# Four-quadrant rows and pixels, Hartley rows stored in their final layout, and a new order of the pieces

## The chip, the cores and the metric

The kernel runs on one core of a Trainium2 chip. The metric is the device time of the program in microseconds; lower is better. The engines named here are PE (matrix products, with PEld for its weight loads), ACT (activations and copies), DVE (vector operations), POOL (GpSimd) and SP, whose queue issues most of the DMA transfers. All data is float32.

## What is computed

Two layers follow each other on an input of 16 images, 64 channels, 128 by 128 pixels. The first is a Hartley convolution: a 2-d Hartley transform, a product with weights on 20 x 20 low modes, the transform back, a Gaussian blur over all four axes, and a mask on the columns. The second is an image network: group norm, a spectral mixer (AFNO) on 32 x 32 modes, a residual, a second group norm, one dense layer of features, two shared experts, and four of sixteen experts per image that a small gate chooses. Cut to what matters:

```python
def _L0_conv_ref(x, w1):
    x_ht = dht_2d(x)
    out_ht = out_ht.at[:, :, :M1, :M2].set(compl_mul2d(x_ht[:, :, :M1, :M2], w1))
    y = gaussian_smoothing_4d(dht_2d(out_ht) / (H * W))
    return y * mask

def _forward(x, ...):
    h = _afno(_group_norm(x, gn1_w, gn1_b), afno_w1, afno_b1, afno_w2, afno_b2) + x
    residual = h
    feats = _gelu(_c1(_group_norm(h, gn2_w, gn2_b), fe_w, fe_b))
    for s in range(shared_w.shape[0]):
        shared = shared + _gelu(_c1(feats, shared_w[s], shared_b[s])) / shared_w.shape[0]
    scores = h2 @ g3_w.T + g3_b          # h2: the gate's layers on the mean of feats
    vals, idx = jax.lax.top_k(scores, TOP_K)
    wts = jax.nn.softmax(vals / TEMPERATURE, axis=1)
    out = shared
    for e in range(NUM_EXPERTS):
        out = out + _gelu(_c1(feats, expert_w[e], expert_b[e])) * gate_w[:, e][:, None, None, None]
    return out + residual
```

## The kernel before

**Stage 1, the transform forward (lines 187 to 266).** Each image is read in eight tiles `xt` and transformed along rows (L250) and, one image later, along columns (L212). DVE adds the result, with the blur over the batch, into `x2` (L231). When an output image is complete, ACT writes its two other halves of `x2` (L236 with a sign, L237 as a copy). The stage is a stream from DRAM of about 330 GB/s.

**Stage 2, modes (lines 268 to 321).** Constants are loaded, `spec` (3.2 MB) and `exw` among them. Eleven steps mix channels per mode (L294) into PSUM tiles `psm`, of which there are two. Each is copied to the two halves of `om`: the lower half by ACT (L298, L301, L302), the upper by DVE (L299, L303). L312 turns them into `ot`, 400 modes in four chunks by image and channel.

**Stage 3, the AFNO loop over 16 images (lines 324 to 567).** After the statistics, every image has eight products of `spec` (L548) and the first layer (L499, L501), whose result goes to DRAM as `o1d` (L503, SP). In the first ten rounds `modes` (L480, L483) also builds `ok`, the Hartley rows of all images on 4 x 32 partitions; in the next four `modes_out` makes a negated copy `onk` (L488) and stores both on POOL's queue to `od` and `ond` (L490, L491), 32 stores of 100 KB with 5,120 B in a row. `prepare` folds the constants; it also makes two rows of bias, `b2r`, and stores them to `b2x`.

**Stage 4, the pieces (lines 570 to 889).** Every image is now worked through in pieces:

- `spectrum` (lines 602 to 611) loads `s` from `o1d` (L606), and the Hartley rows into columns 64 to 104 of `bm` by eight loads (L611). Each row of 20 values is a packet of 80 B.
- `spectrum_f`, twice: 64 products of the second AFNO layer (L622) into one PSUM tile, copied to columns 0 to 63 of `bm` by ACT (L629).
- `rows`, eight times: four channels, four products each (L647), copied to `u` by ACT (L652).
- `pixels`, eight times: for eight rows one product of 107 x 128 x 128 each (L669); ACT adds the residual's shift and writes `h` (L677), DVE takes statistics (L681).
- `norm2` (three steps), `feature` (eight, L732 and L736), and `gate` (eight steps), which ends in a softmax on POOL and DVE and in four gathers of expert weights `wl` (L806).
- `group`, 48 times: four products of 64 x 64 x 512 (L826), a gelu by ACT into `g` (L831), and an addition by DVE into `h` (L834), two shared and four chosen experts for each of eight tiles. After the last expert of a tile its two halves are stored (L845).

All pieces share three PSUM tiles, `pe`, of two banks each. An evacuation is put one piece behind its products, and an addition one further. `PIECES` (line 872 on) holds for each piece its places, counted in groups: piece i of image b stands at `b * 48 + at`, so that a place of -50 means two groups before the end of the image before. The pieces are written out in that order; the framework then orders each queue by what is ready, earlier code first.

```python
        PIECES = (
            (lambda box, i: spectrum(box), (-84,)),
            (spectrum_f, (-57, -50)),
            (feature, (-5, -4, -3, -2, -2, -2, -2, 0)),
            (step("norm", norm2), (-19, -16, -10)),
            (step("gate", gate), (2, 3, 5, 7, 8, 8, 10, 12)),
            (rows, (-50, -49, -48, -48, -48, -40, -39, -38)),
            (pixels, (-36, -32, -28, -24, -24, -24, -23, -23)),
            (group, range(NG)),
        )
```

Of the kernel before, what the change touches and what calls it, by code (L numbers as in the profile page):

```python
# [19 lines left out]
K = 20  # L20
# [9 lines left out]
HR, KC = 52, 105  # L30
KU = KC + 2
# [23 lines left out]
def constant_tables():  # L55
# [23 lines left out]
    inv1, inv2 = np.zeros((128, 2, N)), np.zeros((KU, N))  # L79
# [7 lines left out]
    inv2[KC], inv2[KC + 1] = inv2[:32].sum(0), inv2[32:64].sum(0)  # L87
    c, s = np.cos(a32).sum(0), np.sin(a32).sum(0)
    bias = np.array([[c, s], [-s, c]])

    by_half = lambda t: t.reshape(-1, 2, 2, N // 2).transpose(0, 1, 3, 2).reshape(-1, 2 * N)
    inv1, bias = by_half(inv1), by_half(bias)
# [38 lines left out]
    for loc in range(5):  # L131
# [13 lines left out]
        "bias": bias,  # L145
# [14 lines left out]
def hartley_afno_moe_kernel(ctx: ExitStack, tc: tile.TileContext, a: dict, out: bass.AP):  # L160
# [18 lines left out]
    od = dram.tile([NB, K, C, K], F32, name="od")  # L179
    ond = dram.tile([NB, K, C, K], F32, name="ond")  # L180
# [6 lines left out]
    with tc.tile_pool(name="modes", bufs=1) as mp:  # L187
# [6 lines left out]
        with tc.tile_pool(name="f_x", bufs=10) as xp, tc.tile_pool(name="f_t", bufs=2) as tp, \  # L194
# [9 lines left out]
            def along_columns(b, t1):  # L204
# [20 lines left out]
                for bo in range(NB):  # L225
# [9 lines left out]
                    if not gb[bo, b + 1:].any():  # L235
                        nc.scalar.mul(x2[0:C, 1, bo], x2[C:P, 0, bo], -1.0)  # L236
                        nc.scalar.copy(x2[C:P, 1, bo], x2[0:C, 0, bo])  # L237
# [39 lines left out]
        spec = load(sc, "spec", [CH, 4, 2 * MD * MD])  # L277
        exw = load(sc, "exw", [P, C, NE])

        with tc.tile_pool(name="m_o", bufs=1) as op, \  # L280
# [7 lines left out]
            for k1 in range(K // 2 + 1):  # L288
# [9 lines left out]
                nc.scalar.copy(lok[:, k1], lo[:, :, 0])  # L298
                nc.vector.tensor_copy(upk[:, k1], up[:, :, 0])  # L299
                if k1 % (K // 2):  # L300
                    nc.scalar.copy(lok[:, K - k1, 0:1], lo[:, 0:1, 1])  # L301
                    nc.scalar.copy(lok[:, K - k1, K // 2 - 1:0:-1], lo[:, 1:, 1])  # L302
                    nc.vector.tensor_copy(upk[:, K - k1, ::-1], up[:, :, 1])  # L303
# [18 lines left out]


# [10 lines left out]
    b2 = kp.tile([2, C], F32, name="b2t")  # L334
    for ri in range(2):
        nc.sync.dma_start(b2[ri:ri + 1], a["b2"][32 * ri:32 * ri + 1, 0:C])
    bias = load(kp, "bias", [2, 2, N])
    b2r = kp.tile([P, 2, C], F32, name="b2r")
    b2x = dram.tile([2, N, C], F32, name="b2x")
    inv1 = load(kp, "inv1", [P, 2, N])  # L340
    inv2 = load(kp, "inv2", [KU, N])
# [20 lines left out]
    bm = kp.tile([P, CL, KC], F32, name="bm")  # L362
    nc.gpsimd.memset(bm, 0.0)
# [7 lines left out]
    with tc.tile_pool(name="s_w", bufs=2) as sw, tc.tile_pool(name="s_o", bufs=1) as so, \  # L371
# [15 lines left out]
        ok = so.tile([P, QB, C, K], F32, name="ok")  # L387
        onk = so.tile([P, QB, C, K], F32, name="onk")
        nc.gpsimd.memset(onk, 0.0)
# [83 lines left out]
        def modes(m):  # L473
# [3 lines left out]
            for i in range(2):  # L477
# [6 lines left out]
                ok[:, :, :, 2 * m:2 * m + 2].rearrange("p b c k -> p k (b c)"), ps,  # L484
                st.unsqueeze(1).to_broadcast([P, 2, QB * C]), ALU.mult)

        def modes_out(i):
            nc.scalar.mul(onk[:, i, :, 0:K - 1], ok[:, i, :, 1:K], -1.0)  # L488
            for q in range(4):
                nc.gpsimd.dma_start(od[q * QB + i], ok[q * 32:q * 32 + K, i])  # L490
                nc.gpsimd.dma_start(ond[q * QB + i], onk[q * 32 + 1:q * 32 + 1 + K, i])  # L491
# [14 lines left out]
        def prepare():  # L506
# [8 lines left out]
            ps = pp3.tile([P, 512], F32, name="pso")  # L515
            for i in range(2):
                nc.tensor.matmul(ps[:, i * C:(i + 1) * C], lhsT=bias[:, i], rhs=b2, start=True, stop=True)
            nc.scalar.copy(b2r.rearrange("p i c -> p (i c)"), ps[:, 0:2 * C])
            nc.sync.dma_start(b2x.rearrange("i n c -> n i c"), b2r)
# [50 lines left out]
    with s3:  # L570
        up_, hpp, fp, gp, selp = (pool(n, q) for n, q in (
            ("u", 1), ("hp", 14), ("feats", 9), ("g", 7), ("selw", 2)))
# [5 lines left out]
        nc.sync.dma_start(u[KC:KU], b2x)  # L578
# [22 lines left out]

        def spectrum(box):

            b = box["b"]
            s = box["s"] = sp.tile([P, MD * MD], F32, name="s")
            nc.sync.dma_start(s, o1d[b].rearrange("r c k -> (r c) k"))  # L606
            for h in range(2):
                r, i = (0, 32) if h else (64, 96)
                cs = slice(h * CL, (h + 1) * CL)
                for at, q, src in ((r, 0, od), (i, 1, od), (r + 1, 21, od), (i, 21, ond)):  # L610
                    nc.sync.dma_start(bm[at:at + K, :, 64 + q:64 + q + K], src[b, :, cs, :])  # L611

        def spectrum_f(box, q):
# [13 lines left out]
            def evacuate():  # L627
                bmf = bm[:, :, 0:64].rearrange("p c (r j) -> p r c j", r=2)
                nc.scalar.copy(bmf[:, :, :, q * 16:(q + 1) * 16], ps.rearrange("p i r c -> p r c i"))  # L629
                if q:  # L630
                    box["spectrum"] = True
# [3 lines left out]
        def rows(box, q):  # L635


            if q == 0:
                if "spectrum" not in box:
                    flush()  # L640
            ps = ps2.tile([P, 2, 4, N], F32, name="pe")
            for i in range(4):
                for part, h in ((0, 0), (1, 0), (0, 1), (1, 1)):
                    k0 = C * (h ^ part)
                    rs = slice(k0, k0 + (HR if part else C))
                    cs = slice(64, KC) if part else slice(0, 64)
                    nc.tensor.matmul(ps[cs, h, i, :], lhsT=bm[rs, 4 * q + i, cs],  # L647
                                     rhs=inv1[rs, part], start=True, stop=True)

            def evacuate():  # L650
                dst = u[0:KC].rearrange("p n (h s) -> p h s n", h=2)[:, :, 4 * q:4 * q + 4, :]
                nc.scalar.copy(dst.rearrange("p h s n -> p n h s"),  # L652
                               ps[0:KC].rearrange("p h s n -> p n h s"))
# [4 lines left out]
        def pixels(box, t):  # L658
# [8 lines left out]
            for r in range(8):  # L667
# [292 lines left out]
```

## Time and profile before

| | us |
|---|---|
| median of three runs | 1855.82 (1853.91 to 1858.42) |
| the profiled execution's own time | 1848.89 |
| its span, first to last instruction | 1846.9 |
| stage 1, to the last column product L212 | 253.3 |
| stage 2, to the last L312 | 296.5 |
| stage 3, to the last L501 | 472.4 |
| first row product L647, first group L826 | 478.9, 528.5 |
| first expert activations of images 5 and 10 | 947.9, 1367.6 |
| last group product | 1832.0 |

The profile is of one execution. In the page's lists an entry has the code line, the engine, the operation, the tile written and the tiles read, the shapes and the count; after the bar the busy time, the mean of one in ns, and the idle time before them with what ended it. A list of waits has the waiting instruction, what it waited for, the total in us, how often and the longest. A list by windows has the window and its length, then busy time and count of PE, PEld, DVE, ACT and POOL, the granted clock of PE, the share of DMA and GB/s. A timeline has start, length and instruction. A float32 product shows as two records[...].

### The profile page before, as it was taken

How to read it: one execution, taken by the hardware profiler on the slowest of the kernel's cores; microseconds unless marked ns; L12 is line 12 of the kernel's file. 1: busy time of each engine (PE TensorE's matmuls, PEld its weight loads, DVE VectorE, ACT ScalarE, POOL GpSimd, SP SyncE). 2: the span in 40 equal slices, each digit the busy share in tenths (PEclk: the TensorE clock that was granted, in tenths of full speed). 3: DMA queues.
4: the chain of work that ended last, by engine and by line, in shares of the span. 5: the costliest groups of instructions: out<-in, count | busy, mean ns of one | idle time of the engine just before them, and what ended most of it. 6: DMA issues, size and time to landing. Idle time of an engine off the chain costs nothing. (4 is left out here: it accounts for less than half of the span.)

```text
span 1846.9 us, 55817 instructions
## 1 busy us (share of the span) xinstructions
PE 1701.5 (92%) x24644; PEld 940.8 (51%) x24644; DVE 1270.7 (69%) x1774; ACT 1378.3 (75%) x1690; POOL 120.9 (7%) x140
## 2 busy tenths in 40 slices
PE   6777769999899999999999999999999999999996
PEld 6776765333645455454545555454545455554521
DVE  1233432322249788797979797797979797887988
ACT  2343343112488998989898999989898999989897
POOL 0000002003010101010110101010100101010110
PEclk8899988999999999999999999999999999999998
DMA  9999841115212222222332222322232322222023
GB/s 337 319 322 326 285 145 48 69 52 145 47 25 70 48 81 57 84 36 82 57 72 58 59 82 36 99 41 81 37 86 53 71 72 46 72 57 71 27 72 92
DMA packets 136129, 181.00 MB, mean 98 GB/s; under 512 B 94201, under 2 KB 95414, under 8 KB 135658
## 3 DMA queue, kind: packets, MB, share of 16 engines
q1 hardware_dynamic: 132192, 171.73, 33.1%
q0 software_dynamic: 3696, 5.71, 1.2%
q8 instruction: 193, 3.16, 0.7%
q14 instruction: 48, 0.39, 0.1%
HBM read 98.29 MB, written 79.11 MB: 96 GB/s over the span
## 5 line engine op out<-in xcount | busy, mean ns | idle before, releaser
L834 DVE SCALAR_TENSOR_TENSOR h<-g,wt,h 128x1024 f32<-128x1024 f32 x512 | 620.9, 1275 | 85.2 <-ACT g L831 85.2
L831 ACT ACTIVATE g<-pe,wl 128x1024 f32<-128x1024 f32 x512 | 539.4, 1131 | 8.9 <-PE pe L826 8.2
L826 PE MATMUL pe<-f,wl 64*64 64x512 f32 x4096 | 494.7, 600 | 1.3 <-issue 0.4
L834 DVE SCALAR_TENSOR_TENSOR h<-g,h 128x1024 f32<-128x1024 f32 x256 | 301.6, 1220 | 56.1 <-ACT g L831 56.1
L831 ACT ACTIVATE g<-pe,vec_sb 128x1024 f32<-128x1024 f32 x256 | 278.7, 1135 | 20.6 <-PE pe L826 20.4
L669 PEld LDWEIGHTS pe<-inv_sb,u 107*128 107x128 f32 x2048 | 234.4, 192 | 64.9 <-ACT g L831 33.2
L826 PEld LDWEIGHTS pe<-f,wl 64*64 64x64 f32 x4096 | 135.6, 132 | 237.3 <-ACT g L831 98.6
L826 PE MATMUL pe<-f,shw 64*64 64x512 f32 x2048 | 252.9, 604 | 0.0
L669 PE MATMUL pe<-inv_sb,u 107*128 107x128 f32 x2048 | 248.8, 279 | 3.2 <-ACT g L831 1.9
L677 ACT ACTIVATE h<-pe,gs 128x1024 f32<-128x1024 f32 x128 | 142.6, 1115 | 73.2 <-PE pe L669 57.3
L250 PE MATMUL ps<-fwd_sb,xt 128*64 128x64 f32 x4096 | 141.5, 232 | 51.0 <-issue 43.1
L681 DVE BATCH_NORM_STATS2 stats<-h 128x6 f32<-128x512 f32 x256 | 160.1, 679 | 25.9 <-ACT h L677 25.8
L250 PEld LDWEIGHTS ps<-fwd_sb,xt 128*64 128x64 f32 x4096 | 135.9, 147 | 54.7 <-issue 46.6
L647 PE MATMUL pe<-inv_sb,bm 64*64 64x128 f32 (+1 forms) x4096 | 144.8, 275 | 1.2 <-issue 1.2
L736 ACT ACTIVATE f<-pe,fb 128x1024 f32<-128x1024 f32 x128 | 144.3, 1137 | 2.2 <-PE pe L732 2.2
L647 PEld LDWEIGHTS pe<-inv_sb,bm 64*64 64x64 f32 (+1 forms) x4096 | 118.5, 124 | 48.1 <-ACT f L736 24.3
L253 ACT COPY t<-ps 128x320 f32<-128x320 f32 x128 | 54.0, 427 | 114.4 <-PE ps L250 114.0
L732 PE MATMUL pe<-h,fs 64*64 64x512 f32 x1024 | 133.9, 611 | 1.6 <-DVE n L709 1.6
L652 ACT COPY u<-pe 105x1024 f32<-105x1024 f32 x128 | 127.4, 1043 | 3.9 <-PE pe L647 2.9
L219 DVE TENSOR_TENSOR xm<-ps,pn 64x20 f32<-64x20 f32 x32 | 5.5, 171 | 172.5 <-ACT pn L215 172.2
L548 PE MATMUL psx<-spec_sb,ot 100*64 100x512 f32 x512 | 115.6, 594 | 0.0
L806 POOL DMA_INDIRECT wl<-exd,ati x64 | 66.9, 1045 | 697.4 <-ACT g L831 605.4
(164 smaller groups left out, 1163.5 us busy)
## 6 DMA issues: line engine op xcount, KB each, us to landing
xt<-in_x_dram SPq DMA_DIRECT2D x128, 512.0 KB
out_dram<-h SPq DMA_DIRECT2D x256, 256.0 KB
o1d<-o SPq DMA_DIRECT2D x16, 512.0 KB
s<-o1d SPq DMA_DIRECT2D x16, 512.0 KB
bm<-od SPq DMA_DIRECT2D x96, 50.0 KB
wk<-in_w_dram SPq DMA_DIRECT2D x11, 320.0 KB
wn<-in_w_dram SPq DMA_DIRECT2D x11, 320.0 KB
spec_sb<-in_spec_dram SPq DMA_DIRECT2D x1, 3200.0 KB
```

The costliest lines, as they stand in the source:

```text
L250: nc.tensor.matmul(ps[cols, i, :], lhsT=xt[:, i, cols], rhs=fwd1, start=True, stop=True)
L548: nc.tensor.matmul(ps[ri * C:(ri + 1) * C], lhsT=ot[:, kc, b * C:(b + 1) * C], rhs=spec[:, kc, ri * 1024 + n * 512:ri * 1024 + (n + 1) * 512],
L647: nc.tensor.matmul(ps[cs, h, i, :], lhsT=bm[rs, 4 * q + i, cs], rhs=inv1[rs, part], start=True, stop=True)
L652: nc.scalar.copy(dst.rearrange("p h s n -> p n h s"), ps[0:KC].rearrange("p h s n -> p n h s"))
L669: nc.tensor.matmul(ps[:, r // 4, r % 4 * N:(r % 4 + 1) * N], lhsT=u[0:KU, 2 * row:2 * row + 2, :].rearrange("p h c -> p (h c)"), rhs=inv2, ...
L677: nc.scalar.activation(h, ps, AF.Identity, bias=gs1[:, 1, box["b"]:box["b"] + 1])
L681: nc.vector.bn_stats(box["stats"][:, 2 * t + p, :], h[:, p])
L732: nc.tensor.matmul(ps[p * C:(p + 1) * C, half], lhsT=box["fs"][rows_], rhs=box["h"][t][rows_, p], start=True, stop=True)
L736: nc.scalar.activation(f, ps, AF.Gelu, bias=box["fb"], accum_out=box["sums"][:, t:t + 1])
L826: nc.tensor.matmul(ps[half * C:(half + 1) * C, p], lhsT=w[rows_], rhs=f[rows_, half], start=True, stop=True)
L831: nc.scalar.activation(g, ps, AF.Gelu, bias=bias)
L834: nc.vector.scalar_tensor_tensor(h, g, share(), h, ALU.mult, ALU.add)
```

## The change

**Rows.** The Hartley part of `bm` gets a tile of its own, `bh`, with 41 values per channel behind each other. A channel's rows come from products of 64 columns: both parts, both halves of channels and both halves of pixels, so that each of the four quadrants of the array has one; `inv1` is rearranged accordingly. `u` is now full, 128 partitions.

**Pixels.** For a row, four products of 64 x 64 x 128 for the spectrum, and four of 64 x 64 x 66 for the Hartley part, which add only to the 66 columns that the mask keeps. The rows of bias in `u`, with `bias`, `b2r` and `b2x`, are gone; `b2` is added when the spectrum tile is copied to `bm`, which DVE does now, in two halves.

**Hartley rows.** `ok` has a zero column in front and behind. `modes_out` stores to `odr` and `odi`, per image and row a run of 64 channels x 41 values, with five stores per image on SP's queue; `spectrum` loads each with two long loads.

**Before the images.** The copy L237 goes from ACT to DVE. In stage 2 all five copies of one step are on one engine, ACT and DVE in turn. `spec` and `exw` are loaded after stage 2.

**Order and buffers.** `s` is loaded by a piece of its own. All places change. There are 16 buffers of `h` and 8 of `g` instead of 14 and 7.

```diff
-                        nc.scalar.copy(x2[C:P, 1, bo], x2[0:C, 0, bo])
+                        nc.vector.tensor_copy(x2[C:P, 1, bo], x2[0:C, 0, bo])
...
-                nc.scalar.copy(lok[:, k1], lo[:, :, 0])
-                nc.vector.tensor_copy(upk[:, k1], up[:, :, 0])
+                copy = nc.vector.tensor_copy if k1 % 2 else nc.scalar.copy
+                copy(lok[:, k1], lo[:, :, 0])
+                copy(upk[:, k1], up[:, :, 0])
...
         def modes_out(i):
-            nc.scalar.mul(onk[:, i, :, 0:K - 1], ok[:, i, :, 1:K], -1.0)
+            nc.scalar.mul(onk[:, i, :, 0:K - 1], ok[:, i, :, 2:K + 1], -1.0)
             for q in range(4):
-                nc.gpsimd.dma_start(od[q * QB + i], ok[q * 32:q * 32 + K, i])
-                nc.gpsimd.dma_start(ond[q * QB + i], onk[q * 32 + 1:q * 32 + 1 + K, i])
+                r, b = q * 32, q * QB + i
+                for to, frm in (
+                    (odr[b, :, :, 0:K + 1], ok[r:r + K + 1, i, :, 1:K + 2]),
+                    (odr[b, 1:, :, K + 1:], ok[r:r + K, i, :, 1:K + 1]),
+                    (odr[b, 0:1, :, K + 1:], ok[r + K:r + K + 1, i, :, 1:K + 1]),
+                    (odi[b, :, :, 0:K + 1], ok[r:r + K, i, :, 0:K + 1]),
+                    (odi[b, :, :, K + 1:], onk[r + 1:r + 1 + K, i]),
+                ):
+                    nc.sync.dma_start(to, frm)
...
+        def spectrum_in(box):
+            s = box["s"] = sp.tile([P, MD * MD], F32, name="s")
+            nc.sync.dma_start(s, o1d[box["b"]].rearrange("r c k -> (r c) k"))
+
         def spectrum(box):
             b = box["b"]
-            s = box["s"] = sp.tile([P, MD * MD], F32, name="s")
-            nc.sync.dma_start(s, o1d[b].rearrange("r c k -> (r c) k"))
             for h in range(2):
-                r, i = (0, 32) if h else (64, 96)
                 cs = slice(h * CL, (h + 1) * CL)
-                for at, q, src in ((r, 0, od), (i, 1, od), (r + 1, 21, od), (i, 21, ond)):
-                    nc.sync.dma_start(bm[at:at + K, :, 64 + q:64 + q + K], src[b, :, cs, :])
+                for at, n, src in ((h * C, K + 1, odr), (h * C + 32, K, odi)):
+                    nc.sync.dma_start(bh[at:at + n, 0:CL * HC],
+                                      src[b, :, cs, :].rearrange("k c j -> k (c j)"))
...
-                bmf = bm[:, :, 0:64].rearrange("p c (r j) -> p r c j", r=2)
-                nc.scalar.copy(bmf[:, :, :, q * 16:(q + 1) * 16], ps.rearrange("p i r c -> p r c i"))
+                bmf = bm.rearrange("p c (r j) -> p r c j", r=2)
+                for i in (0, 8):
+                    j = q * 16 + i
+                    nc.vector.tensor_tensor(bmf[:, :, :, j:j + 8],
+                                            ps[:, i:i + 8].rearrange("p i r c -> p r c i"),
+                                            b2.unsqueeze(3).to_broadcast([P, 2, CL, 8]), ALU.add)
...
-                for part, h in ((0, 0), (1, 0), (0, 1), (1, 1)):
-                    k0 = C * (h ^ part)
-                    rs = slice(k0, k0 + (HR if part else C))
-                    cs = slice(64, KC) if part else slice(0, 64)
-                    nc.tensor.matmul(ps[cs, h, i, :], lhsT=bm[rs, 4 * q + i, cs],
-                                     rhs=inv1[rs, part], start=True, stop=True)
+                for part in range(2):
+                    for h, p in ((0, 0), (1, 1), (1, 0), (0, 1)):
+                        rs = slice(h * C, h * C + (HR if part else C))
+                        c = 4 * q + i
+                        nc.tensor.matmul(ps[p * C:(p + 1) * C, h, i, part, :],
+                                         lhsT=bh[rs, c * HC:c * HC + C] if part else bm[rs, c],
+                                         rhs=inv1[rs, part, p * C:(p + 1) * C], start=True, stop=True)
...
-            for r in range(8):
-                row = t * 8 + r
-                nc.tensor.matmul(
-                    ps[:, r // 4, r % 4 * N:(r % 4 + 1) * N],
-                    lhsT=u[0:KU, 2 * row:2 * row + 2, :].rearrange("p h c -> p (h c)"),
-                    rhs=inv2, start=True, stop=True)
+            quadrants = ((0, 0), (1, 1), (0, 1), (1, 0))
+            for r in range(4):
+                n = 2 * (4 * t + r)
+                for p, half in quadrants:
+                    k = slice(p * C, (p + 1) * C)
+                    nc.tensor.matmul(ps[half * C:(half + 1) * C, p, r * N:(r + 1) * N],
+                                     lhsT=u[k, n + half, :], rhs=inv2[k, 0:N], start=True, stop=False)
+                for p, half in quadrants:
+                    k = slice(p * C, (p + 1) * C)
+                    to = ps[half * C:(half + 1) * C, p, r * N:(r + 1) * N]
+                    nc.tensor.matmul(bass.AP(to.tensor, to.offset, [to.ap[0], (N - MH, 2), (1, MH)]),
+                                     lhsT=u[k, C + n + half, :],
+                                     rhs=inv2[k, N:].rearrange("k (a n) -> k a n", a=2),
+                                     start=False, stop=True)
...
-            (lambda box, i: spectrum(box), (-84,)),
-            (spectrum_f, (-57, -50)),
-            (feature, (-5, -4, -3, -2, -2, -2, -2, 0)),
-            (step("norm", norm2), (-19, -16, -10)),
-            (step("gate", gate), (2, 3, 5, 7, 8, 8, 10, 12)),
-            (rows, (-50, -49, -48, -48, -48, -40, -39, -38)),
-            (pixels, (-36, -32, -28, -24, -24, -24, -23, -23)),
+            (lambda box, i: spectrum_in(box), (-92,)),
+            (lambda box, i: spectrum(box), (-86,)),
+            (spectrum_f, (-76, -73)),
+            (feature, (-9, -8, -8, -7, -5, -5, -2, -1)),
+            (step("norm", norm2), (-23, -19, -14)),
+            (step("gate", gate), (1, 2, 3, 4, 5, 6, 9, 11)),
+            (rows, (-60, -59, -48, -45, -43, -41, -39, -39)),
+            (pixels, (-34, -33, -33, -32, -31, -30, -29, -26)),
```

## The prediction, made before the changed kernel ran

> **What bounds the kernel now.** I read the page first, then busy time by windows of 100 us, then the waits between 1000 and 1700 us, then the timelines of TensorE and of SP's queue.
>
> ```profile
> span 1846.9 us, 55817 instructions
> PE 1701.5 (92%) x24644; PEld 940.8 (51%) x24644; DVE 1270.7 (69%) x1774; ACT 1378.3 (75%) x1690; POOL 120.9 (7%) x140
> ```
> ```profile
> 1400.00:1500.00 100.00, 97.50 (x1248) 53.69 (x1252) 86.70 (x110) 90.02 (x100) 5.55 (x6) 1.00 0.28 65
> ```
> ```profile
> DVE h L834 <- ACT g L831: 83.9, 34, 5.9
> ACT h L677 <- PE pe L669: 26.6, 46, 0.8
> DVE den L812 <- POOL dv L799: 21.8, 8, 2.7
> ```
> In the middle of the run PE is busy 97.5%, ACT 90%, DVE 87% of the time: three engines close together, PE first. One image takes 83.6 us (the first of its 48 expert activations starts at 947.9, the next image's at 1032.3; ten images lie between 83.3 and 84.4). In a stretch of pure expert groups ACT sets the pace (one L831 per 1.00 us, PE needs 0.86); at the pixels PE does, and ACT waits for L669.
>
> ```profile
> 1064.79 5.62 PE L669 MATMUL pe<-inv_sb,u 107*128 107x128 f32 x48
> 1070.35 1.09 PE L826 MATMUL pe<-f,wl 64*64 64x512 f32 x8
> ```
> ```profile
> 1041.07 1.10 PE L647 MATMUL pe<-inv_sb,bm 64*64 64x128 f32 x32
> 1041.99 1.04 PE L826 MATMUL pe<-f,shw 64*64 64x512 f32 x8
> ```
> Three pixel tiles hold PE from 1064.79 to 1070.35: 1.78 us each and 0.2 at the change to another shape. A row tile (32 records, eight sets of four quadrants) takes 0.92 from its start to the next piece, 0.109 a set.
>
> **What the Trainium skill says.** "TensorEngine Tiling (Array Packing)", Key Properties: 64x64 tiles run independently, and a change of tiling mode drains the engine. The trace agrees: four 64x64x512 matmuls (8 records) take 0.86 together, and a lone pixel tile takes 1.98 (1047.75 to 1049.73) where one in a row takes 1.78. "VectorE: DVE Perf Modes", Side-by-side: one element a cycle at 0.96 GHz plus about 158 cycles for a two-source operation; for 512 elements an estimate of (512+158)/0.96 = 0.70 us. The trace has 64x200 from PSUM at 369 ns (L222), near it, and one that is far off (L483, below). "DMA: Bandwidth & Descriptors", Specifications: under 512 B a transfer is a read-modify-write. The trace has such short packets only on the reading side of DRAM.
>
> **The change, part by part.**
>
> Pixels. Today 8 matmuls of 107x128x128 per tile. After: 4 times (four quadrants of N 128, then four of N 66). A set with N 128 is the row tile's, 0.109 for each of two passes; one with N 64 runs in the spectrum piece L622, whose sets start 0.055 apart (1017.38, 1017.43, 1017.49). A tile is 4 x (0.218 + 0.110) = 1.31 instead of 1.78: 3.8 us per image, and about 0.4 more where the pixels no longer change the mode (five such places per image, 0.1 each).
>
> Rows. Eight sets of N 128 per tile (four channels, two passes) become sixteen of N 64: 16 x 0.055 = 0.88 against 8 x 0.109 = 0.87; 0.1 us per image. The evacuation writes 128 partitions for 105, same free size: nothing (L652, 1.04).
>
> Spectrum evacuation. ACT loses L629, two of 1.056 per image (2.1 us); DVE gains four additions of 512 from PSUM.
>
> ```profile
> L629 ACT COPY bm<-pe 128x1024 f32<-128x1024 f32 x32 | 33.8, 1056 | 12.3 <-PE pe L622 12.0
> L483 DVE TENSOR_TENSOR ok<-psd,st 128x512 f32<-128x512 f32 x10 | 12.2, 1222 | 12.3 <-PE psd L480 12.3
> L222 DVE TENSOR_TENSOR xm<-ps,pn 64x200 f32<-64x200 f32 x32 | 11.8, 369 | 0.4
> ```
> From below 0.70 each, from above L483's 1.22, which writes elements 80 B apart. The new one writes runs of 8; I take 0.70: 2.8 us per image, 4.9 at the upper end. DVE's load per image rises from about 75 us (85.5% of 83.6, and 3.4 of waits for POOL) to 78, under 80 at the worst. It isn't the bound yet, but two of PE's three PSUM tiles now wait behind DVE's queue: the pieces stand at groups 20 and 23, where an addition of today starts 2.1 to 3.0 us after its activation has ended. Counting from the end of a spectrum tile: DVE still has an addition and a pair of statistics (ends +1.55), then the two additions (+2.95); PE wants that buffer after two expert groups (+1.8). PE stands about 1.1 at the first and little at the second: 1.3 us per image, 0.2 to 3.5 as bounds.
>
> Order. Gate steps are a group apart instead of one or two: today's stalls there (0.84 and 0.73 us of PE per image) stay as they are. Features and rows leave the stretch in which ACT was already full; ACT, relieved by 2.1, isn't the bound there for more than 0.3. More h buffers (14 to 16) take away 8 us of waits for out stores in the whole run, hidden by PE: nothing.
>
> Sum per image: -4.2 + 0.1 + 1.3 + 0.3 = -2.5 us; 15 intervals, **-37**. Image 0's lead-in (472 to 530, PE 50 of 58 us busy) saves its own pixels: **-3.5**. The tail of the last image is pure experts at DVE's 1.20 per addition: nothing.
>
> Before the images. The last x2 copies: ACT alternates L236 and L237, ten of 0.53, until 261.4, while DVE ends at 257.9; with five on DVE both end near 259.4: -2. The mode mixing:
>
> ```profile
> 261.40:289.80 28.40, 20.55 (x442) 19.45 (x442) 9.38 (x26) 10.27 (x35) 0.43 (x1) 0.74 0.59 158
> ```
> ```profile
> DVE om L299 <- ACT om L298: 14.3, 9, 6.3
> ```
> ACT and DVE copy the same PSUM tile in turns, and PE runs at a clock of 0.74. With a whole tile per engine (five copies, 2.0 us) and two tiles in flight, a step is between 1.7 and 2.3 us instead of 2.6; eleven steps: -5 (-3 to -9), and -1 in L312 behind it. Spec is now asked for after this stage: 3.2 MB at the 330 GB/s of the first slices is 10 us from 289, wanted at L548, 320.9: hidden with 20 us to spare. Together **-8**.
>
> Hartley rows. Today 32 long stores on POOL's queue, and eight loads an image in 80 B packets, hidden. After: 80 stores on SP's queue in pieces of 80 and 84 B, 5,248 packets an image, all ready at once when ok is complete (420), and four long loads an image.
>
> ```profile
> 338.39 0.33 SPq L606 DMA_DIRECT2D s<-o1d  x1
> ```
> ```profile
> 425.36 0.32 SPq L503 DMA_DIRECT2D o1d<-o  x1
> 425.73 4.04 SPq L611 DMA_DIRECT2D bm<-od  x2
> 429.87 4.39 SPq L611 DMA_DIRECT2D bm<-ond  x1
> 434.35 1.84 SPq L503 DMA_DIRECT2D o1d<-o  x1
> ```
> ```profile
> 1046.14 1.31 SPq L611 DMA_DIRECT2D bm<-od  x3
> 1047.49 0.60 SPq L611 DMA_DIRECT2D bm<-ond  x1
> 1048.19 2.16 SPq L611 DMA_DIRECT2D bm<-od  x3
> 1050.39 0.72 SPq L611 DMA_DIRECT2D bm<-ond  x1
> ```
> SP's order isn't the program's (s of image 0 at 338, in the middle of the loop that stands before it): what is ready goes, earlier code first. All 80 stores stand in the code ahead of image 0's loads, which can be ready only after the first five. So the loads for the first rows probably sit behind all of them. The price: 640 packets cost SP 0.62 us in steady state (4.97 us for 5,120), so 16 images are 16 x 5,248 x 0.97 ns = 81 us. Start 420 - 8 = 412, end 493, o1d stores between them 5, loads and landing 3: first rows at 501, instead of 478.9 - 8 = 471. PE stands about **+33** between loop and first rows; nothing else is there to do. Bounds: 0, if the loads slip in between or short packets go faster; 60 and more, if SP, in order, stands waiting for each next o1d with stores behind it (around 425 it placed three or four loads between two of them), or if a short write is dearer than a short read (at twice the price 110).
>
> Sum: 1848.9 (the profiled execution; its span is 1846.9) - 37 - 3.5 - 8 + 33 = 1833. The median of the runs shown is 6.9 above that execution: **1840**.
>
> **Rivals.** B, no stall at the start: the 80 stores drain under the AFNO loop. For it: the loop has 52 us left after ok is complete, and DMA is nearly idle there; against it, 81 us of SP. Time 1807. C, the slower side: the stores hold back the first rows by more than the 49 us won elsewhere. One mechanism, SP's queue between 412 and the first bh load, deciding from a stall of 49 us; at 60 us the time is 1867, at 110 it is 1917. For it: SP stood long on such loads near 430 (up to 4.4 us each), and the read-modify-write. Against: those stood beside POOL's stores, which go. D, DVE takes PE's place as the bound: additions at 1.22, lag at groups 20 and 23 above 3 us, the PSUM buffer held 3 us and more twice an image. The image stays at 83.6 or so, and the time is 1877 with the stall, 1844 without.
>
> **How the numbers follow.** About 0.2% (3.7 us) is what a measurement can tell from no change. My forecast (stall of 20 to 49 us) 0.36, B 0.24, C 0.30, D 0.10. Faster: 0.32 of the forecast, all of B, 0.02 of D, so 0.58; same 0.04 of the forecast and 0.02 of C, 0.06; slower the rest, 0.36. The likeliest case alone reaches from 1827 to 1856; the range from 1793 (B with a little more per image) to 1900 (C at a stall of 90) leaves out 0.2.
>
> **What would show it.** A gap of PE between the last L499 and the first row matmul of about 30 us, with SP issuing stores all through it; rows and pixels at 0.9 and 1.3 us; an image at 81.1; DVE additions into bm at 0.7; psm to om steps of 2 us. It is wrong if the first bh load goes out before 470, if it goes out after 520, or if an image takes over 83 or under 79 us.

## The result, and the profile after

The changed kernel takes 2040.95 us (2040.65 to 2044.54), the kernel before 1856.57 in the same comparison: a ratio of 1.100, with a 95% interval from 1.098 to 1.102. It was forecast at 1840. Its profiled execution takes 2040.84, with a span of 2039.1. Below, a total whose ratio to the kernel before is given with an interval is the median of 4 to 22 executions. Every other total is one execution, so small differences rest on the mean length of an image within it.

The page of the changed kernel, its first two lines, and the rows of TensorE's busy share and granted clock (40 slices of 51 us, in tenths):

```profile
span 2039.1 us, 76261 instructions
PE 1685.6 (83%) x34880; PEld 907.9 (45%) x34880; DVE 1328.7 (65%) x1859; ACT 1332.1 (65%) x1638; POOL 129.9 (6%) x109
...
PE   6777779991001799999999999999999999999996
...
PEclk8899979996555899999999999999999999999998
```

PE did slightly less work than before (1685.6 against 1701.5 us), yet its share fell from 92% to 83%: there is a hole in the tenth to thirteenth slice. The view by windows (start and end, length, then busy time and count of PE, PEld, DVE, ACT and POOL, PE's clock, DMA share, GB/s) shows what was busy in it:

```profile
450.00:550.00 100.00, 21.26 (x82) 5.97 (x78) 3.87 (x7) 2.53 (x4) 0.00 (x0) 0.60 0.74 41
550.00:650.00 100.00, 3.68 (x8) 0.77 (x8) 0.00 (x0) 1.27 (x2) 0.00 (x0) 0.50 0.83 40
...
1137.90:1892.80 754.90, 720.40 (x15718) 358.75 (x15714) 660.43 (x838) 673.82 (x767) 64.48 (x54) 1.00 0.23 65
```

From 450 to 650 us the engines hardly worked, and the DMA engines were 74 to 83% busy to move only 40 GB/s. SP's queue, from its timeline (start, length, instruction), says with what:

```profile
418.38 3.14 SPq L503 DMA_DIRECT2D odr<-ok  x2
423.28 0.35 SPq L515 DMA_DIRECT2D o1d<-o  x1
423.69 0.58 SPq L503 DMA_DIRECT2D odr<-ok  x1
424.32 0.82 SPq L503 DMA_DIRECT2D odi<-ok  x1
425.24 3.31 SPq L503 DMA_DIRECT2D odi<-onk  x1
```
```profile
640.44 2.15 SPq L503 DMA_DIRECT2D odi<-onk  x1
642.69 4.55 SPq L515 DMA_DIRECT2D o1d<-o  x2
647.29 0.73 SPq L620 DMA_DIRECT2D bh<-odr  x1
```

The 80 Hartley stores hold SP from 418.4 to 642.7, 224 us or 14.0 an image, and only then does the first load of `bh` go out, at 647.3. The group list of the page shows a second victim of the same queue: a store of `o1d` goes out at 423.3, behind the first two of these, and then at 471.1, 528.5, 585.0 and 642.7, behind twenty more each time, and the AFNO loop's activation waits for them before it can write its tile `o` again.

```profile
L513 ACT ACTIVATE o<-pso,b 128x512 f32<-128x512 f32 x32 | 21.6, 687 | 304.2 <-DMA o1d<-o 210.0
```

Where the 192.2 us between the two spans lie, by the starts of the first row product and of each image's first expert activation (g below):

| us | before | after | difference |
|---|---|---|---|
| first row product | 478.9 | 661.5 | +182.6 |
| from there to g of image 0 | 51.2 | 58.0 | +6.8 |
| fifteen images, g of 0 to g of 15 | 1248.8 | 1250.1 | +1.3 |
| from g of image 15 to the end | 68.0 | 69.5 | +1.5 |

So there are two questions: why the stores took 224 us, and why fifteen images gained nothing where 37 us were forecast. For the second, TensorE's time per image, counted for each kind of piece from its start to the start of what follows (twelve images in the middle; a wait of TensorE so counts with the piece before it):

| us an image | before | after |
|---|---|---|
| pixels | 15.27 | 12.74 |
| rows | 7.91 | 8.09 |
| transforms to the spectrum | 3.88 | 4.74 |
| features | 7.53 | 8.25 |
| groups | 46.65 | 47.53 |

The pixels save 2.5, and the other pieces together take it back. Waits of the changed kernel over nine images (1137.9 to 1892.8; waiting instruction, what it waited for, total us, times, longest):

```profile
PEld pe L688 <- issue: 38.8, 83, 2.8
...
ACT h L701 <- PE pe L693: 29.3, 27, 3.6
...
PE pe L688 <- DVE bm L641: 12.1, 9, 2.0
```

Once an image a pixel tile stands because the PSUM tile it needs is still being read by VectorE's addition (L641), up to 2.0 us; ScalarE then starves behind it (up to 3.6).

### The profile page after: what moved, and what is told of

It is laid out like the page before. It is cut to its first block, busy times and chain, and to the rows that moved or that the text cites. A ratio compares the mean times of both kernels' runs of the same rounds, so it can differ in the third digit from the quotient of the medians.

```text
span 2039.1 us, 76261 instructions
## 1 busy us (share of the span) xinstructions
PE 1685.6 (83%) x34880; PEld 907.9 (45%) x34880; DVE 1328.7 (65%) x1859; ACT 1332.1 (65%) x1638; POOL 129.9 (6%) x109
## 5 line engine op out<-in xcount | busy, mean ns | idle before, releaser
L855 ACT ACTIVATE g<-pe,wl 128x1024 f32<-128x1024 f32 x512 | 562.1, 1175 | 67.6 <-PE pe L850 64.8
L850 PE MATMUL pe<-f,wl 64*64 64x512 f32 x4096 | 521.8, 602 | 4.7 <-issue 0.8
L688 PE MATMUL pe<-inv_sb,u 64*64 64x128 f32 x4096 | 202.1, 274 | 26.3 <-DVE bm L641 19.5
L513 ACT ACTIVATE o<-pso,b 128x512 f32<-128x512 f32 x32 | 21.6, 687 | 304.2 <-DMA o1d<-o 210.0
L688 PEld LDWEIGHTS pe<-inv_sb,u 64*64 64x64 f32 x4096 | 160.0, 135 | 85.8 <-issue 66.5
L693 PE MATMUL pe<-inv_sb,u 64*64 64x66 f32 x4096 | 177.4, 220 | 5.0 <-issue 5.0
L693 PEld LDWEIGHTS pe<-inv_sb,u 64*64 64x64 f32 x4096 | 167.4, 135 | 8.8 <-issue 8.8
L641 DVE TENSOR_TENSOR bm<-pe,b2t 128x512 f32<-128x512 f32 x64 | 41.0, 681 | 174.0 <-PE pe L632 174.0
L668 ACT COPY u<-pe 128x1024 f32<-128x1024 f32 x128 | 134.4, 1065 | 22.5 <-PE pe L662 18.5
L511 PE MATMUL pso<-xk,wc 128*64 128x512 f32 x128 | 37.8, 682 | 124.4 <-ACT o L513 123.9
L662 PE MATMUL pe<-inv_sb,bm 64*64 64x64 f32 x4096 | 135.6, 224 | 5.8 <-issue 3.2
```

What stands on the lines that cost most here:

```text
L662: nc.tensor.matmul(ps[p * C:(p + 1) * C, h, i, part, :], lhsT=bh[rs, c * HC:c * HC + C] if part else bm[rs, c], rhs=inv1[rs, part, p * C:( ...
L668: nc.scalar.copy(dst.rearrange("p h s n -> p n h s"), ps.rearrange("p h s a n -> p (a n) h s"))
L688: nc.tensor.matmul(ps[half * C:(half + 1) * C, p, r * N:(r + 1) * N], lhsT=u[k, n + half, :], rhs=inv2[k, 0:N], start=True, stop=False)
L693: nc.tensor.matmul(bass.AP(to.tensor, to.offset, [to.ap[0], (N - MH, 2), (1, MH)]), lhsT=u[k, C + n + half, :], rhs=inv2[k, N:].rearrange( ...
L850: nc.tensor.matmul(ps[half * C:(half + 1) * C, p], lhsT=w[rows_], rhs=f[rows_, half], start=True, stop=True)
L855: nc.scalar.activation(g, ps, AF.Gelu, bias=bias)
```

## The experiments

My theory after this result was that the whole loss is the price of the short stores, and that the images gain nothing since a transform's tile is held in PSUM behind VectorE's queue. The rivals were, for the start, that SP's order rather than the price of the runs does it, and for the images, that ScalarE's load, TensorE itself or the new places do it.

**The stores taken back alone.** POOL stores `ok` and `onk` as long rows, and `bh` is filled by short runs.

```diff
-                for to, frm in (... five stores ...):
-                    nc.sync.dma_start(to, frm)
+                nc.gpsimd.dma_start(od[b], ok[r:r + K, i])
+                nc.gpsimd.dma_start(ond[b], onk[r + 1:r + 1 + K, i])
...
+                for at, j, n, src in ((h * C, 0, K + 1, od[b, :, cs, 1:]), (h * C + 1, K + 1, K, od[b, :, cs, 1:K + 1]),
+                                      (h * C + 32, 0, K + 1, od[b, :, cs, 0:K + 1]), (h * C + 32, K + 1, K, ond[b, :, cs, :])):
+                    nc.sync.dma_start(to[at:at + K, :, j:j + n], src)
```

> The Hartley rows are stored again as long rows by POOL's queue (od 5,632 B, ond 5,120 B a row), and bh is filled by eight loads of 80 and 84 B runs an image, as bm was before; all the rest is as in the changed kernel. If the short stores are the whole loss (of the 184 us, and images gain nothing), 1848 to 1862 us, first rows near 470 us, first group near 528 us, an image still 83.7 us. If part of the loss comes from elsewhere (the order's earlier pieces, the pixel or row tiles in image 0), it stays above 1880. If the stores also slow the images through the DMA engines, an image falls to 81 to 82 us and the time to 1810 to 1830.

1860.28 us, a ratio of 1.002 to the kernel before (1.000 to 1.004). The first row product is at 478.3 and an image takes 83.7 (the mean of 14 intervals, here and below). The stores are the whole loss, and they don't slow the images. This kernel is the base of the experiments on the images below. SP's queue in it:

```profile
422.56 0.31 SPq L616 DMA_DIRECT2D bh<-od  x1
424.48 0.32 SPq L509 DMA_DIRECT2D o1d<-o  x1
424.85 4.91 SPq L616 DMA_DIRECT2D bh<-od  x2
429.86 5.95 SPq L616 DMA_DIRECT2D bh<-ond  x1
```

Image 0's loads go out 2.8 us after the first long store (419.77 on POOL).

**Another queue for the short stores**, and **another queue for `o1d`**:

```diff
-                    nc.sync.dma_start(to, frm)
+                    nc.gpsimd.dma_start(to, frm)
```
```diff
-                nc.sync.dma_start(o1d[b].rearrange("r c k -> (r c) k"), o1)
+                nc.gpsimd.dma_start(o1d[b].rearrange("r c k -> (r c) k"), o1)
```

> The same 80 stores in short runs go out on POOL's queue instead of SP's. If SP's in-order queue is what costs (what stands behind the stores waits, while DMA engines have room), the loop with L513 runs free, and only image 0's own five stores count: 1850 to 1880 us. If the packets themselves are the price (84,000 packets fill the DMA engines or the queue), the first load of bh comes no earlier than before by more than some tens of us: 1960 to 2050. If POOL issues short runs more slowly than SP does, later still: over 2050.

> Only the 16 stores of o1d move to POOL's queue; the Hartley stores stay on SP. If the loss is the wait of L513 for its tile o between the batches of stores, the loop is through by 475 us and the time falls with it to 1870 to 1900. If the loss is SP's queue up to the first load of bh, the loop is through by 475 us all the same, but the first load still goes out at 630 to 645 us: 2020 to 2040, a gain of 0 to 20 us.

2009.84 and 2022.8 us. With the short stores on POOL's queue the AFNO loop ran through (last L513 at 486.3), image 0's loads went out at 438.9 and its rows began at 500.3, all as SP's order would have it (these rows then took 44 us, where they take 17 in the changed kernel). But the DMA engines needed the same time, from 426.5 to about 650, and the wait only moved:

```profile
ACT h L701 <- DMA odi<-onk: 106.4, 1, 106.4
```

The tile `h` that the pixels write lies in memory that `onk` held, and stays taken until the last store has read it. With `o1d` alone on POOL's queue the loop was through at 474.8, but:

```profile
635.73 3.25 SPq L503 DMA_DIRECT2D odi<-onk  x1
639.02 2.52 SPq L620 DMA_DIRECT2D bh<-odr  x1
```
```profile
PE pe L662 <- DMA bh<-odi: 165.4, 2, 164.5
```

The stores took 216 us without any `o1d` between them. So the wait of L513 for `o1d`, the largest in the page, cost no more than 18 of the 184 us; taking it away lets the next wait in the chain end last. The price of the runs is the cause, and whoever uses that data or that memory pays it.

**What the price is per.** First the five stores to four tensors of their own, where the runs lie close behind each other; then two stores an image of 62 runs of 164 B a row. The second reads `ok` with overlap, leaves two channels of 64 out and has wrong values in the last 20 of a row.

```diff
-                    (odr[b, :, :, 0:K + 1], ok[r:r + K + 1, i, :, 1:K + 2]),
-                    (odr[b, 1:, :, K + 1:], ok[r:r + K, i, :, 1:K + 1]),
+                    (odr[b], ok[r:r + K + 1, i, :, 1:K + 2]),
+                    (odm[b, 1:], ok[r:r + K, i, :, 1:K + 1]),
...
```
```diff
-                for to, frm in (... five stores ...):
+                nc.sync.dma_start(odr[b, :, 0:C - 2], wide(r, K + 1, 1))
+                nc.sync.dma_start(odi[b, :, 0:C - 2], wide(r, K, 0))
```

> The changed kernel, with its five stores an image going to four tensors of their own, in which each run of 84 or 80 B follows closely on the one before (pitch 84 or 80 B; the negated part 84), instead of lying interleaved at a pitch of 164 B; the loads of bh become short runs. The number and size of the written runs and the queue stay. If the price is that of the runs: the stores still take 190 to 225 us, and 2000 to 2045 in all. If it is that of runs which share lines of memory with others at a wide pitch: the stores take 80 to 120 us, 1890 to 1940.

> The changed kernel with two stores an image in place of five: each writes 62 runs of 164 B a row (41 floats read from ok with overlap, so that the last 20 of a row hold wrong values, two channels in 64 are left out, and the outputs are not the reference's). 40,700 runs in place of 83,968, 6.7 MB in place of 6.9. If the price is a run's: the stores take 100 to 115 us, the first group comes at 590 to 610, 1910 to 1935 in all. If it is a byte's: 205 to 225 us, 2020 to 2045. If it is that of two stores whose runs meet in one row: under 60 us, under 1890.

2092.89 and 1975.22 us.

| stores | runs | us from first to last | ns a run |
|---|---|---|---|
| changed kernel, SP, 80 and 84 B at a pitch of 164 | 83,968 | 418.4 to 642.7 | 2.67 |
| the same, `o1d` on POOL | 83,968 | 422.7 to 639.0 | 2.58 |
| close behind each other | 83,968 | 417.9 to 697.2 | 3.33 |
| 164 B | 40,672 | 423.9 to 577.7 | 3.78 |
| for comparison, loads of 80 B before (one image) | 5,120 | 1047.04 to 1053.40 | 1.24 |

Lying close behind each other didn't help the runs; it made them a quarter dearer, which neither branch of the expectation had. Half as many runs of twice the length took 69% of the time, between the branches of the other: the price is neither a run's alone nor a byte's alone. What is firm is that a run on its way to DRAM took 2.6 to 3.8 ns in each form tried, and one on its way from DRAM 1.2 to 1.5 (fifteen images of the kernel before and of the one with long stores; image 0's loads, which go out among other transfers, apart). The backlog of stores doesn't make the difference: the first 5,248 runs of the changed kernel, with none ahead of them, already took 13.0 us, 2.5 ns each. Whether writing short runs in DRAM or reading them from SBUF is what is dear, no run here separates.

**Which engine bounds an image.** Three kernels on the base, each with less work for one engine: ScalarE copies half of a row tile to `u` (the other half stays zero); VectorE takes the statistics of half of the pixels; TensorE leaves out the pixels' second pass.

```diff
-                dst = u.rearrange("p n (h s) -> p h s n", h=2)[:, :, 4 * q:4 * q + 4, :]
+                dst = u.rearrange("p n (h s) -> p h s n", h=2)[:, :, 4 * q:4 * q + 4, 0:C]
```
```diff
-                    for p in range(2):
-                        nc.vector.bn_stats(box["stats"][:, 2 * t + p, :], h[:, p])
+                    nc.vector.bn_stats(box["stats"][:, t, :], h[:, 0])
```
```diff
-                for p, half in quadrants:
-                    k = slice(p * C, (p + 1) * C)
-                    to = ps[half * C:(half + 1) * C, p, r * N:(r + 1) * N]
-                    nc.tensor.matmul(bass.AP(...), ..., start=False, stop=True)
```

> On the first experiment's kernel (long stores, new places, 1860 us, an image 83.7 us), ScalarE copies only one half of each row tile into u; the other half of u stays at zero, so those outputs lose the low-rank part. ScalarE has some 0.45 us less for each of 8 tiles, 3.6 us an image. If ScalarE's own load is what eats the pixels' gain: 80 to 81 us an image, 1815 to 1825 in all. If it is VectorE's hold on PSUM or the tensor engine itself: 83 to 83.7, 1850 to 1860. If the load of the three engines is level and their order loses the rest: 82 to 83.

> On the same kernel, VectorE takes the statistics of every second row of pixels only, 8 x 0.6 = 4.8 us an image less (the normalization is then over half of the pixels). If VectorE's backlog, and through it the PSUM buffer that the transform's evacuation holds, eats the gain: 80 to 82 us an image, 1815 to 1835. If ScalarE is the bound: no change, 83.5 to 83.9, 1855 to 1862.

> On the same kernel, the pixel tiles' second pass (66 columns, 16 matmuls a tile) is left out, so that the pixels lack the low-rank part: 0.5 to 0.6 us of TensorE for each of 8 tiles, 4 to 5 us an image. If TensorE still sets the pace: 79 to 80 us an image, 1800 to 1810. If a dearer pixel tile was no bound any more, as the lost 4.2 us of the forecast suggest: 83 to 83.7, 1850 to 1860.

| less work for | us an image less, measured | an image, us (mean of 14) | time |
|---|---|---|---|
| none (base) | | 83.7 | 1860.28 |
| ScalarE | 2.7 | 82.5 | 1838.81 |
| VectorE | 4.0 | 82.2 | 1837.66 |
| TensorE | 3.7 | 84.3 | 1864.11 |

Less for TensorE brings nothing, and neither of the others gives back half of what it is relieved of: no one of the three is the bound alone. VectorE's and TensorE's results lie just above the ranges that I had expected, 80 to 82 us and 83 to 83.7. With the second pass gone, the pixels took 9.04 us of TensorE an image instead of 12.7, but the groups 51.9 instead of 47.3. The wait of the pixels for VectorE's addition grew from 1.3 us an image (12.1 over nine, above) to 3.8:

```profile
PE pe L683 <- DVE bm L636: 34.5, 9, 4.0
```

Of the 3.7 us that TensorE saves, 2.5 come back as this wait for the held tile.

**The held tile.** ScalarE copies the transform's tile, without the bias; then the bias added in SBUF after that copy, by POOL or by VectorE.

```diff
-                    nc.vector.tensor_tensor(bmf[:, :, :, j:j + 8], ps[:, i:i + 8].rearrange("p i r c -> p r c i"), ..., ALU.add)
+                nc.scalar.copy(bmf[:, :, :, at], ps.rearrange("p i r c -> p r c i"))
+                for j in (q * 16, q * 16 + 8):
+                    to = bmf[:, :, :, j:j + 8]
+                    nc.vector.tensor_tensor(to, to, b2.unsqueeze(3).to_broadcast([P, 2, CL, 8]), ALU.add)
```

> On the same kernel, ScalarE takes the transform's tiles to bm, with one copy of 1.02 us each as in the kernel before, and the bias is not added. VectorE loses 4 x 0.61 = 2.5 us an image, ScalarE gets 2.0 more. If VectorE's hold on PSUM eats the gain: 81 to 82.5 us an image, 1820 to 1840, and no pixel or row tile waits for bm. If ScalarE's load eats it: 84 to 86 us, 1865 to 1890.

> The kernel with long stores, new places, and ScalarE copying the transform's tiles to bm; the bias is then added in bm by POOL, two pieces of 128x512 a tile, out of PSUM's way (13 groups lie between the second transform and the first rows). If it is the PSUM buffer held behind VectorE that ate the pixels' gain, POOL's additions cost nothing: 81.5 to 82 us an image, 1833 to 1842, which beats both kernels. If POOL's additions slow VectorE[...], 82.5 to 83.5, 1845 to 1858.

> The same, but VectorE adds the bias in bm (SBUF to SBUF): its load is as in the changed kernel, and no PSUM buffer waits for it. If the buffer held is the price: 81.5 to 82.5 us an image, 1835 to 1845. If VectorE's load of 2.5 us an image is: 83 to 84, 1855 to 1865.

> The kernel of the look at 1839 us again (long stores; ScalarE copies the transform's tiles to bm, VectorE adds the bias in SBUF), timed: 1836 to 1845 us if its 81.8 us an image hold, a ratio of 0.990 to 0.995 to the kernel before; 1850 or more if the look was a lucky one.

Without the bias an image takes 81.7 us (1835.12 in all). With VectorE's addition in SBUF it is 81.9 (1839.1, and 1842.13 as the median of six); VectorE's load is the changed kernel's again, so it was not the load but the tile held in PSUM. How long it is held, the traces show: in the changed kernel VectorE starts on the first of an image's two transform tiles 2.1 us after its last product, and is done with it after 3.3 (1.9 with the second tile). ScalarE, in this kernel without the bias as in the kernel before, starts after 0.07 and is done after 1.1. With less for TensorE, VectorE is done with the first tile after 5.7 only (medians of twelve images). The waits of the kernel with VectorE's addition in SBUF over nine images (786.7 to 1524.1), beside those of the changed kernel above:

```profile
PEld pe L683 <- issue: 26.2, 85, 0.8
ACT bm L635 <- PE pe L627: 18.3, 18, 1.6
...
ACT h L696 <- PE pe L688: 15.7, 10, 2.1
```
```profile
786.70:1524.10 737.40, 712.38 (x15718) 356.94 (x15714) 658.39 (x838) 690.64 (x785) 64.44 (x54) 1.00 0.28 67
```

TensorE's products no longer wait for `bm` at the pixels (their weights do for 0.3 us an image), the longest wait of a pixel tile's weights falls from 2.8 to 0.8 us, and ScalarE, which has 2 us more to do an image, is now 94% busy (690.64 of 737.40) against 89% (673.82 of 754.90). POOL is the worse place for the addition: 82.6 us an image and 1847.61, a ratio of 0.997 (0.995 to 0.998). Its additions took 1.05 to 2.15 us each, VectorE's 0.68, and they slowed VectorE: its additions into `h` that overlapped one of them took 1.78 us on average, the others 1.25. In twelve images 60 did, which is 2.6 us more work for VectorE per image, about what it was relieved of.

The kernel with VectorE's addition in SBUF, at 0.994 (0.992 to 0.996) of the kernel before, is the best of the case: it has the change's quadrants and places, the old storage, and the addition out of PSUM's way.

**The places.** The base with the places of the kernel before; the same with ScalarE's copy and no bias; and the kernel before with the new places and the new numbers of `h` and `g` tiles.

```diff
-            (spectrum_f, (-76, -73)),
-            (feature, (-9, -8, -8, -7, -5, -5, -2, -1)),
+            (spectrum_f, (-57, -50)),
+            (feature, (-5, -4, -3, -2, -2, -2, -2, 0)),
...
```

> The long stores of the first experiment, and with them the places that the kernel before gave its pieces in the image loop (spectrum -84, transforms -57 and -50, features -5 to 0, and so on); quadrant rows and pixels and VectorE's evacuation of bm stay. If the new places eat the pixels' gain (features close together with ScalarE as the bound), an image takes 81 to 82 us: 1810 to 1830. If VectorE's evacuation holds PSUM and eats it, an image stays at 83.5 to 85: 1845 to 1870, and the wait of pixel or row tiles for bm stays about as large.

> Long stores, quadrant rows and pixels, ScalarE copying the transform's tiles without the bias, and the old places in the image loop; beside the run with the same pieces at the new places (81.7 us an image, 1835). If the new places themselves bring something: 82.5 to 84 us here, 1845 to 1865. If they only make room for VectorE's evacuation, the same 81 to 82, 1825 to 1840. The old places with VectorE's evacuation took 92.5 us.

> The kernel before with the changed kernel's places in the image loop and its numbers of h and g tiles (16 and 8), nothing else of the change. If the new places alone bring the gain of 1.9 us an image: 81.5 to 82.2 us, 1828 to 1840. If the quadrant pixels are needed for it (1.9 us of TensorE less a pixel tile would then count): 83.3 to 85, 1850 to 1880.

| us an image | old places | new places |
|---|---|---|
| products and evacuation of before | 83.7 (before) | 85.2 (1885.22) |
| quadrants, ScalarE's copy, no bias | 86.6 (1898.14) | 81.7 (1835.12) |
| quadrants, VectorE's addition from PSUM | 92.7 (1983.81) | 83.7 (base) |

At the old places VectorE's addition costs far more than I expected (a ratio of 1.068, 1.064 to 1.072), and the other two kernels also came out slower than their expectations. With that addition at the old places the groups themselves wait for it, and ScalarE and VectorE starve for up to 6 us at a time (nine images, 908.9 to 1744.9):

```profile
DVE h L853 <- ACT g L850: 130.7, 79, 5.7
ACT g L850 <- PE pe L845: 89.2, 64, 6.0
...
PE pe L845 <- DVE bm L636: 42.7, 9, 5.2
```

Quadrants and places belong together: either alone makes an image slower than before, by 1.5 us (places) or 2.9 (quadrants), and both together 2 us faster, once the tile isn't held (1.8 with the bias added). Why the quadrants are slower than the old pixels at the old places even with ScalarE's copy was not followed further. Of the 1885.22 us, some 15 come from a later start of the modes, before any place matters.

## Why the prediction was wrong

**The step that failed: "16 images are 16 x 5,248 x 0.97 ns = 81 us".** The count of packets was right, and so was the queue: all 80 stores stood ahead of image 0's loads. The price was taken from reads of short runs on SP's queue; a written run took 2.67 ns, 2.75 times as much. The upper bound written beside it, "at twice the price 110", was short of that too. The first rows, forecast at 501, came at 661.5: a stall of 190 us against rows at 471, where the range reached to 90. (The sum carried +33; its own times, 501 less 471, give 30.) It is rival C's mechanism in its place, and both the price and the bound were too small. The stores of `o1d` between them, put at 5 us, cost 8 (224 us with them, 216 without). The Trainium skill says that a transfer under 512 B is a read-modify-write ("DMA: Bandwidth & Descriptors", Specifications), without a price. The prediction quoted it and still priced a write like a read. The runs are in keeping with it, 1.2 to 1.5 ns for a run read from DRAM and 2.6 to 3.8 for one written, but that a read-modify-write is what makes them dear is not shown by any run here.

**The image: "-2.5 us each".** The operations were sized well: a pixel tile took 1.33 to 1.35 us (forecast 1.31), a row tile 0.96 to 0.98 (0.88), an addition 0.68 (0.70). What failed is "three engines close together, PE first", behind the sum: taking 3.7 us more of TensorE away made an image 0.6 us slower, so TensorE's time saved was no gain in itself. The term "PE stands about 1.1 at the first and little at the second: 1.3 us per image" gave the direct wait rightly (1.3 measured), and its +2.95 for the hold fits the first tile's 3.3 above, though not the second's 1.9. But ScalarE's starving behind the held tile and the longer groups weren't in it. Putting the addition behind a copy brought 1.8 us an image, and the groups fell from 47.5 to 46.1 us; the price of the hold is probably more than 1.8, since ScalarE does 2.0 us more there.

The hold is not all that was missing. Without its 1.3 the forecast would have been -3.8, and the image gained 1.8. Nor can the order be summed as a term of its own, "+0.3": the new places cost the kernel before 1.5 us an image and bring the quadrants with ScalarE's copy 4.9. Part of what is missing are the features, which take 8.3 us of TensorE at the new places whether the tile is held (8.25), free (8.26) or the pixels are the old ones (8.31), against 7.5 before. Rival D (0.10) named the held tile and the 83.6 us, but not by its path: VectorE did not become the bound (4.0 us less for it gave 1.5), its additions took 0.68 instead of 1.22, and of the two tiles an image only one was held over 3 us.

**Image 0's lead-in: "saves its own pixels: -3.5".** The pixels of image 0 saved nothing, 14.9 us against 14.5, and the lead-in became 6.8 longer; in the kernel with the old storage it is 5.9 longer too. The prediction gave the rows +0.1 an image and counted nothing for them here. From the first row product to the first pixel product:

| us | old places | new places |
|---|---|---|
| row products of before | 10.4 (before) | 10.7 |
| quadrant row products | 16.8 (ScalarE's copy) | 17.0 (changed kernel and base) |

So the new row products take 6 us more there, and the order has no part in it. A row tile takes 2.1 us in this stretch and 0.98 in the middle of the run. TensorE stands before these products for 5.7 us (3.2 in the base, 1.2 before) in gaps that the profile puts down to nothing ("issue"), and for 1.4 us behind the addition into `bm`. What the gaps are stays open.

**Before the images: "-8".** The modes took 26.6 us (260.5 to 287.1) against 27.8 before, and 26.8 to 30.0 in the other kernels with this code: no gain. A whole tile for one engine didn't make the step shorter. With the long stores the first row product stood at 478.3, against 478.9 before: of the 8 us nothing is left. TensorE's timeline of the changed kernel in this stage (in brackets the idle time before and what ended it):

```profile
271.40 2.53 PE L290 MATMUL psm<-x,wk 128*64 128x64 f32 x78 [1.35 <-DVE om L301]
...
278.06 2.76 PE L290 MATMUL psm<-x,wk 128*64 128x64 f32 x80 [0.71 <-ACT om L301]
...
284.93 2.19 PE L290 MATMUL psm<-x,wk 128*64 128x64 f32 x36 [3.17 <-issue]
```

TensorE still waits for the last copy of a tile (L301), from either engine, and the longest gap is one that no copy ends ("issue"). That gap of some 3 us stood there before as well; what it is stays open. The start of this stage alone moved between 256.5 and 276.1 from kernel to kernel; why was not followed.

**The tail: "nothing"**: +1.5, near enough.

## What to carry to other kernels

When a layout has to be changed on the way through DRAM, put the short runs where DRAM is read, and where there is time in steady state: here eight short loads an image lay hidden beside 83 us of work, the short stores came all at once with nothing beside them. Before moving an evacuation to another engine, look at what stands in that engine's queue: here the PSUM tile was held for the queue (2.1 us) and then for the operation, and a plain copy out with the arithmetic done later in SBUF can be cheaper though it is more work. When three engines are each over 85% busy, relieve each by a known amount before believing that the fullest is the bound, and change the order of the pieces together with their lengths.

## What the runs showed that I had not expected

The median packet was as quick when written as when read, 12 ns; the means are 31.9 (short stores of the changed kernel) and 16.2 (loads of one image before). The dearness lies in a tail: 7% of the written packets took over 50 ns and made up 64% of all their time, 1.6% and 13% in the loads. On POOL's queue the runs travel up to 49 in one packet, yet a packet of 49 runs of 84 B (4,116 B) took 1.38 us on average, 28 ns a run, about as much as on SP. And an addition of 128x512 within SBUF took POOL 1.77 us (median) beside a busy VectorE, and VectorE 0.68; where the two overlapped, VectorE's own additions of 128x1024 went from 1.25 to 1.78 us.
